# Moving three batches' 3x3 convolution and gate from the opening to the step ahead of the preceding batch's attention

## The chip, the cores and the metric

The kernel runs on one core of one Trainium2 chip. The metric is the time of one execution on the device in microseconds (us). Three executions of the kernel before took 5047.65, 5047.94 and 5053.58 us; the median is 5047.94 us.

## What is computed

The input x has 8 batches of 384 channels by 32x32 pixels (1024 tokens), all float32. Layer 0 normalizes each token over its channels (xn), runs a selective scan (a Mamba block) over the tokens forward and backward, and adds a gated depthwise convolution:

```
x_norm      = rmsnorm(x) * norm_w
global_feat = scale_mod * (mamba(x_norm) + flip(mamba(flip(x_norm))))
conv        = depthwise 3x3 convolution of x_norm            # per channel, over the 32x32 image
local_feat  = sigmoid(conv + dw_b) * x_norm
x           = x + res_scale * (global_feat + local_feat)
```

Layer 1 takes the tokens of that x through causal attention with 6 heads, and then, for batches 0 to 4, through a feed-forward block with sign-binarized weights whose activations are quantized with one maximum per batch. Only `local_feat` and the addition to x are computed in another place by the change.

## The kernel before, in words

A batch has 3 chunks of 128 channels (one channel per partition) and 2 halves of 512 tokens, so a tile of one chunk and half is 128x512 and fills one PSUM bank. PSUM's eight banks are handed out by tag: "s" and "pt" two each, "da" two, "y" and "av" one each (`BANKS`). Tiles of 128x1024 in SBUF come from a pool "mid" of 10 buffers, whole-batch tiles from a pool "big" of 6.

A batch passes through these stages:

- `before_scan` (L307): x is loaded (L320), normalized (L326 to L334), projected in `in_proj` (L336), convolved along the tokens in `conv` (L350) and passed through Silu; `local` (L383) makes the 3x3 convolution and `gates` (L444) the gate and the residual; `delta` (L511) makes the step sizes that the scan takes. Results are spilled to DRAM: u, us, z, "t" (x plus the local part) and the delta tiles.
- the scan: 96 units per batch (`Unit`, L544), each for two of the 16 states of one chunk, half and direction. A unit is a multiply on GpSimd (L588), two exponentials on ScalarE (L601), two scans on VectorE (L606), a second multiply on GpSimd (L612) and eight TensorE transposes that sum into PSUM (L620). `slot` (L1100) issues the parts of successive units, so that the first multiply of a unit is issued two slots ahead of its scans (`AHEAD`).
- `attention` (L674): loads of the scan's output and of "t", output projection (L695, added to "t" at L703), layer norm, q and k (L725), v (L743); from here on scores, softmax and weighted values; last the projection `ap` (L934). Up to and with v this text calls it the front of an attention.
- `feed_forward` (L968), for batches 0 to 4, spread together with `before_scan` of a batch still to come.

Every stage is a list of steps with a cost in us written by hand (`Steps`, L1074). `spread_over` (L1083) merges lists in proportion to the sums of their costs. First `before_scan` of batch 0 runs alone (`begin`, L1138). Then comes the opening: the slots of batch 0's 96 units are spread over one list, `beside` (L1137 to L1145), which holds batch 0's z projection and gates, the binarizing of both weights, and `before_scan` of batches 1, 2 and 3. Last comes the main part: the slots of the other seven batches are spread over `rest` (L1148 to L1157), in which follow for each batch its attention and its feed-forward; the due points of L1151 see to it that a batch's units are issued before its attention. After the last slot only the attention of batch 7 is left. From the lists a scheduler makes one fixed order per engine, and each engine takes its instructions in that order; `tc.high_priority` pulls some forward, `pin` keeps the order of some as written. All loads and spills named here are issued from SyncE's queue (`load`, L111; `spill`, L123), also in a fixed order.

For one chunk and half, `local` copies xn times the middle tap into a PSUM bank on ScalarE (L389) and adds the other eight taps with eight VectorE operations (L400), each reading and writing the bank. `gates` then applies tanh on ScalarE (L453), since sigmoid(v) = 0.5 + 0.5 tanh(v/2), and two VectorE operations: times xn (L460) and times half of res_scale plus x (L463).

In `local` and `gates` both halves of a chunk hold a bank of the tags "s" and "pt" in the opening, which the projections use too.

Of the kernel before, what the change touches and what calls it, by code (L numbers as in the profile page):

```python
# [22 lines left out]
NH = L // HB  # L23
# [20 lines left out]
HURRY = 400  # L44
AHEAD = 2
ORDER = (0, 1, 2, 3, 5, 6, 4, 7)
LOG_EXP = "natural_log_exp_and_others"


# [5 lines left out]
def kernel(  # L55
# [49 lines left out]
    def half(h):  # L105
        return slice(h * HB, (h + 1) * HB)
# [4 lines left out]
    def load(dst, src):  # L111
        nc.sync.dma_start(out=dst, in_=src)
# [10 lines left out]
    def spill(key, src, name):  # L123
        d = dram.tile([P, L], F32, name=name, tag="sp_" + "_".join(str(k) for k in key[1:]))
        nc.sync.dma_start(out=d, in_=src)
        spilled[key] = d
# [177 lines left out]
                    )  # L304


    def before_scan(b, tags, emit, later=None, diags=None):  # L307


        st = {}  # L310
# [2 lines left out]
        def bank_of(name):  # L313
            return bank(name, next(turns))
# [8 lines left out]
        for h in range(NH):  # L323

            @emit
            def _(h=h):  # L326
                sqs = squares(st["xn"], h, f"n0_{b}")
                ms = mean_of(lambda c: sqs[c], f"ms_{b}_{h}")
                rstd_of(ms, 0)
                for c in range(NC):  # L330
                    xc = st["xn"][:, c, half(h)]
                    nc.vector.scalar_tensor_tensor(
                        xc, xc, vec[:, c, V_NORM : V_NORM + 1], ms, ALU.mult, ALU.mult
                    )  # L334

        def in_proj(c, i, h):  # L336
            if i == 1 and h == 0:
# [42 lines left out]
                st["u", d, c][:, half(h)], acc, AF.Identity, bias=vec[:, c, V_CB : V_CB + 1]  # L380
            )

        def local(c, h):  # L383

            acc = bank_of(f"loc_{b}_{c}_{h}")
            r0, rows = h * (HB // W), HB // W
            img = acc.rearrange("p (i j) -> p i j", j=W)
            src = st["xn"][:, c, :].rearrange("p (i j) -> p i j", j=W)
            nc.scalar.activation(  # L389
                acc, st["xn"][:, c, half(h)], AF.Copy, scale=vec[:, c, V_DW + 4 : V_DW + 5]  # L390
            )
            for k in range(9):
                di, dj = k // 3 - 1, k % 3 - 1
                if k == 4:
                    continue
                i0, i1 = max(r0, -di), min(r0 + rows, H - di)
                j0, j1 = max(0, -dj), W - max(0, dj)
                to = img[:, i0 - r0 : i1 - r0, j0:j1]
                tap = src[:, i0 + di : i1 + di, j0 + dj : j1 + dj]
                nc.vector.scalar_tensor_tensor(  # L400
                    to, tap, vec[:, c, V_DW + k : V_DW + k + 1], to, ALU.mult, ALU.add
                )
            return acc
# [11 lines left out]
        for c in range(NC):  # L415

            @emit
            def _(c=c):
                st["up", c] = mtile(f"up_{b}_{c}")
                for d in range(2):  # L420
                    st["u", d, c] = mtile(f"u{d}_{b}_{c}")
                if c + 1 < NC:
                    weights_of(c + 1)

            for i, to in enumerate((emit, emit if later is None else later)):
                for h in range(NH):
                    to(lambda c=c, i=i, h=h: in_proj(c, i, h), 2.6)
            for d in range(2):
                for h in range(NH):
                    emit(lambda c=c, d=d, h=h: conv(c, d, h), 3.0)  # L430

            def silus(ts):
                for t in ts:
                    pin(nc.scalar.activation(t, t, AF.Silu))

            def sum_of_us(c=c):
                usum = mtile(f"us_{b}_{c}")
                nc.vector.tensor_tensor(usum, st["u", 0, c], st["u", 1, c], ALU.add)
                spill((b, "us", c), usum, f"sus_{b}_{c}")
                for d in range(2):  # L440
                    spill((b, "u", d, c), st["u", d, c], f"su_{d}_{b}_{c}")


            def gates(c=c, silus=silus, sum_of_us=sum_of_us):  # L444
                st["xc"] = mtile(f"xc_{b}_{c}")
                load(st["xc"], x[b, chunk(c), :])
                accs = [local(c, h) for h in range(NH)]
                with tc.high_priority(offset=60):
                    us = [st["u", 0, c], st["u", 1, c]] if later is None else []
                    silus(us + [st["z", c]])  # L450
                    for h in range(NH):
                        pin(
                            nc.scalar.activation(  # L453
                                accs[h], accs[h], AF.Tanh, scale=0.5, bias=dwbh[:, c : c + 1]
                            )
                        )
                    pin(nc.scalar.preload_act_table_set(LOG_EXP))
                for h in range(NH):
                    acc, xc = accs[h], st["xc"][:, half(h)]
                    nc.vector.scalar_tensor_tensor(  # L460
                        acc, acc, 1.0, st["xn"][:, c, half(h)], ALU.add, ALU.mult
                    )
                    nc.vector.scalar_tensor_tensor(xc, acc, rsh, xc, ALU.mult, ALU.add)  # L463
                spill((b, "t", c), st["xc"], f"st_{b}_{c}")
                spill((b, "z", c), st["z", c], f"sz_{b}_{c}")
                if later is None:
                    sum_of_us()

            def gates_of_us(c=c, silus=silus, sum_of_us=sum_of_us):
                with tc.high_priority(offset=60):  # L470
                    silus([st["u", 0, c], st["u", 1, c]])
                    pin(nc.scalar.preload_act_table_set(LOG_EXP))
                sum_of_us()

            if later is None:
                emit(gates, 14.0)
            else:
                emit(gates_of_us, 4.0)
                later(gates, 10.0)


            for h in range(NH):

                def project(c=c, h=h):
                    xp = bank_of(f"xp_{b}_{c}_{h}")
                    for d in range(2):
                        nc.tensor.matmul(
                            out=xp[d * DW : (d + 1) * DW, :],
                            lhsT=wx[:, c, :],
                            rhs=st["u", d, c][:, half(h)],  # L490
                            start=True,
                            stop=True,
                        )
                    xd = st["xd"][:, half(h)]
                    if c == 0:
                        nc.scalar.activation(xd, xp, AF.Identity, bias=onerow)
                    else:
                        nc.vector.tensor_tensor(xd, xd, xp, ALU.add)

                emit(project)  # L500
# [170 lines left out]
        spilled[b, "gy", c, h] = t  # L671


    def attention(b, emit_ffn, emit):  # L674
        st = {}

        @emit
# [55 lines left out]
        for j in range(NT):  # L733

            @emit
            def _(j=j):
                if j == 0:
                    st["v"] = btile(f"v_{b}").rearrange("p c l -> p (c l)").rearrange(
                        "p (j e) -> p j e", e=C
                    )  # L740
                vp = bank(f"vp_{b}_{j}")
                for c in range(NC):
                    nc.tensor.matmul(  # L743
                        out=vp[:, :C],
                        lhsT=st["xn"][:, c, chunk(j)],
                        rhs=wv[:, c, :],
                        start=(c == 0),
                        stop=(c == NC - 1),
                    )
                nc.any.tensor_copy(st["v"][:, j, :], vp[:, :C])  # L750

        @emit
        def _():
# [361 lines left out]
    def steps_of(stage, *args, **kwargs):  # L1115
        out = Steps()
        stage(*args, out, **kwargs)
        return out
# [19 lines left out]
    begin = Steps()  # L1138
    before_scan(ORDER[0], ("s", "pt"), begin, beside)
    run(begin)  # L1140
    beside += steps_of(before_scan, ORDER[1], ("s", "pt"), diags=diags)
    beside += steps_of(binarize, w1, w1s, NC, FF, 2, "w1")
    beside += steps_of(binarize, w2, w2s, NF, C, 8, "w2")
    for b in ORDER[2 : 1 + ahead]:
        beside += steps_of(before_scan, b, ("s", "pt"), diags=diags)  # L1145
    run(first, beside)

    rest, later, due = [], list(ORDER[1 + ahead :]), [(0.0, 0)]  # L1148
    for i, b in enumerate(ORDER):
        if i > 0:  # L1150
            due.append((sum(us for _, us in rest), i * per))  # L1151
        fed = Steps()
        rest += steps_of(attention, b, fed) if i < B - 1 else []
        if fed and later:
            fed = spread_over(fed, steps_of(before_scan, later.pop(0), ("pt", "pt", "av")))
            fed = [(f, JOINT * us) for f, us in fed]
        rest += fed  # L1157
# [65 lines left out]
```

## Time and profile before

| | us |
|---|---|
| median of three executions | 5047.94 |
| the profiled execution, whole | 5051.18 |
| its span, first to last instruction | 5049.4 |
| TensorE busy | 4101.8 |
| VectorE busy | 3599.9 |
| GpSimd busy | 3691.4 |
| ScalarE busy | 2721.4 |
| first scan multiply (L588) starts | 127 |
| first output projection of attention (L695) starts, batch 0 | 831 |
| the same, in the order of batches 1, 2, 3, 5, 6, 4, 7 | 1496, 2170, 2867, 3551, 3913, 4281, 4840 |
| first scores (L786) start, batches 0, 1, 2 | 924, 1610, 2284 |

The stretch 127 to 831 is the opening, 831 to 4840 the main part, and from 4840 on the last attention runs without scans. "Busy" is the time in which an engine executes, merged where instructions overlap. PE is TensorE's matmul, PEld its weight load, DVE VectorE, ACT ScalarE, POOL GpSimd and SP SyncE. L followed by a number is a line of the kernel before.

### The profile page before, as it was taken

How to read it: one execution, taken by the hardware profiler on the slowest of the kernel's cores; microseconds unless marked ns; L12 is line 12 of the kernel's file. 1: busy time of each engine (PE TensorE's matmuls, PEld its weight loads, DVE VectorE, ACT ScalarE, POOL GpSimd, SP SyncE). 2: the span in 40 equal slices, each digit the busy share in tenths (PEclk: the TensorE clock that was granted, in tenths of full speed). 3: DMA queues.
4: the chain of work that ended last, by engine and by line, in shares of the span. 5: the costliest groups of instructions: out<-in, count | busy, mean ns of one | idle time of the engine just before them, and what ended most of it. 6: DMA issues, size and time to landing. Idle time of an engine off the chain costs nothing. (4 is left out here: it accounts for less than half of the span.)

```text
span 5049.4 us, 50760 instructions
## 1 busy us (share of the span) xinstructions
PE 4101.8 (81%) x16458; PEld 2191.0 (43%) x16458; DVE 3599.9 (71%) x4780; ACT 2721.4 (54%) x4891; POOL 3691.4 (73%) x1944
## 2 busy tenths in 40 slices
PE   4687787878788888788787888888888978878899
PEld 1243343544434444444443444434444544444444
DVE  6887978667786777876678867678767666666523
ACT  4565665565645656545556446565365455464426
POOL 0578687987669886778876788768788978877710
PEclk7788797989889899888998889898888989989999
DMA  6554646324363334453234633335543334324210
GB/s 230 197 176 158 207 156 226 113 86 144 135 210 117 115 114 163 156 174 125 103 129 143 208 109 127 114 116 191 174 131 115 104 99 141 106 92 132 89 64 26
DMA packets 365010, 696.36 MB, mean 138 GB/s; under 512 B 30104, under 2 KB 88904, under 8 KB 364744
## 3 DMA queue, kind: packets, MB, share of 16 engines
q1 hardware_dynamic: 355232, 676.97, 39.7%
q10 hardware_dynamic: 9512, 16.15, 0.9%
q8 instruction: 130, 2.13, 0.2%
q14 instruction: 136, 1.11, 0.1%
HBM read 527.33 MB, written 165.68 MB: 137 GB/s over the span
## 5 line engine op out<-in xcount | busy, mean ns | idle before, releaser
L588 POOL TENSOR_TENSOR g<-ud,bc 128x1024 f32<-128x1024 f32 x768 | 1839.3, 2395 | 652.0 <-PE y L620 513.1
L612 POOL TENSOR_TENSOR g<-g,bc 128x1024 f32<-128x1024 f32 x768 | 1820.5, 2371 | 228.4 <-DVE g L606 175.6
L601 ACT ACTIVATE da<-dl,amat 128x512 f32<-128x512 f32 x1536 | 1056.1, 691 | 1481.1 <-DVE g L606 1438.6
L606 DVE TENSOR_TENSOR_SCAN g<-da,carry,g 128x512 f32<-128x512 f32 x768 | 957.6, 1271 | 405.7 <-POOL g L588 364.7
L606 DVE TENSOR_TENSOR_SCAN g<-da,g 128x512 f32<-128x512 f32 x768 | 906.4, 1210 | 472.7 <-POOL g L588 439.9
L620 PE MATMUL y<-ident,g 128*128 128x128 f32 x6144 | 932.4, 299 | 270.7 <-POOL g L612 214.6
L620 PEld LDWEIGHTS y<-ident,g 128*128 128x128 f32 x6144 | 772.5, 154 | 729.1 <-POOL g L612 339.9
L786 PE MATMUL s<-k,q 64*128 64x512 f32 (+3 forms) x1152 | 405.1, 610 | 122.9 <-DVE nm L800 111.5
L800 DVE CUSTOM_DVE_ANT_0 pr<-s,cmask 128x512 f32<-128x512 f32 (+3 forms) x576 | 300.6, 545 | 212.6 <-PE s L786 185.8
L810 ACT ACTIVATE pr<-pr,nm 128x512 f32<-128x512 f32 (+3 forms) x576 | 348.8, 606 | 141.7 <-DVE nm L800 139.5
L862 PE MATMUL pt<-ident,pr 128*128 128x128 f32 x1728 | 301.9, 305 | 73.5 <-ACT ptn L864 32.9
L993 PE MATMUL hp<-t,w 128*128 128x512 f32 x720 | 339.4, 617 | 27.1 <-DMA w<-w1s 15.2
L1038 PE MATMUL yp<-h,w 128*128 128x512 f32 x720 | 329.2, 615 | 10.3 <-DMA w<-w2s 5.5
L341 PE MATMUL in<-xn,win 128*128 128x512 f32 x576 | 293.3, 651 | 46.3 <-DVE xc L463 14.8
L862 PEld LDWEIGHTS pt<-ident,pr 128*128 128x128 f32 x1728 | 209.1, 153 | 237.2 <-ACT ptn L864 88.6
L875 PE MATMUL av<-ptn,v 128*64 128x512 f32 (+3 forms) x1152 | 276.6, 563 | 23.9 <-DVE o L889 16.2
L864 ACT COPY ptn<-pt 128x512 f32<-128x512 f32 (+3 forms) x576 | 255.2, 474 | 74.0 <-PE pt L862 72.6
L725 PE MATMUL qp<-t,wqk 128*128 128x512 f32 x576 | 263.9, 608 | 17.5 <-DVE t L302 12.0
L400 DVE SCALAR_TENSOR_TENSOR loc<-xn,vec,loc 128x496 f32<-128x496 f32 (+3 forms) x384 | 260.4, 721 | 24.2 <-ACT loc L389 22.7
L611 POOL COPY carry<-g 128x2 f32<-128x2 f32 x384 | 85.8, 224 | 248.1 <-DVE g L606 248.1
L786 PEld LDWEIGHTS s<-k,q 64*128 64x128 f32 x1152 | 138.4, 208 | 251.8 <-DVE nm L800 187.6
L1038 PEld LDWEIGHTS yp<-h,w 128*128 128x128 f32 x720 | 140.3, 199 | 178.9 <-issue 166.3
(155 smaller groups left out, 4809.8 us busy)
## 6 DMA issues: line engine op xcount, KB each, us to landing
bc<-rows SPq DMA_DIRECT2D x512, 512.0 KB, 4.1
dl<-sdl SPq DMA_DIRECT2D x160, 256.0 KB, 2.9
ud<-sud SPq DMA_DIRECT2D x160, 256.0 KB, 2.7
t<-st SPq DMA_DIRECT2D x63, 512.0 KB, 5.3
su<-u SPq DMA_DIRECT2D x48, 512.0 KB, 3.8
du<-su SPq DMA_DIRECT2D x96, 256.0 KB, 4.5
sdl<-du SPq DMA_DIRECT2D x96, 256.0 KB, 2.4
sud<-du SPq DMA_DIRECT2D x96, 256.0 KB, 2.8
```

The costliest lines, as they stand in the source:

```text
L341: nc.tensor.matmul(out=mp, lhsT=st["win", c][:, k, i, :], rhs=st["xn"][:, k, half(h)], start=(k == 0), stop=(k == NC - 1),)
L588: pin(nc.gpsimd.tensor_tensor(g, ud, sst["bc", 0, u.b, u.part, u.n], ALU.mult))
L601: nc.scalar.activation(da, sst["dl", u.b, u.c, u.part], AF.Exp, scale=amat[:, u.c, n : n + 1])
L606: nc.vector.tensor_tensor_scan(gi[:, ::step], da[:, ::step], gi[:, ::step], first, ALU.mult, ALU.add)
L612: pin(nc.gpsimd.tensor_tensor(g, g, sst["bc", 1, u.b, u.part, u.n], ALU.mult))
L620: nc.tensor.matmul(out=y[:, j, :], lhsT=g[:, i, chunk(j)], rhs=ident, is_transpose=True, start=(u.opens and i == 0 and j == 0), stop=(u.cl ...
L786: mm = nc.tensor.matmul(out=ss[e][:, : k1 - k0], lhsT=st["q"][rows_of(e), c, chunk(qi)], rhs=st["k"][rows_of(e), c, k0:k1], start=True, st ...
L800: nc.vector.tensor_tensor_reduce(out=x, in0=ss[e][:, :w], in1=mask, scale=-1.0, scalar=-MASKED, op0=ALU.add, op1=ALU.min, accum_out=m,)
L810: nc.scalar.activation(x, x, AF.Exp, bias=m, scale=-1.0, accum_out=rs[:, i, e, kb : kb + 1])
L862: nc.tensor.transpose(pt[:, chunk(i)], pr[:, e, chunk(j % QT)], ident)
L993: nc.tensor.matmul(out=hp, lhsT=st["w1"][:, c, chunk(m % 2)], rhs=st["xn"][:, c, half(h)], start=(c == 0), stop=(c == NC - 1),)
L1038: nc.tensor.matmul(out=yp, lhsT=st["w2", k // 6][:, k % 6, :], rhs=st["h", k // NC][:, k % NC, half(h)], start=(k == 0), stop=(k == NF - 1),)
```

## The change

`before_scan` gets a list `apart`, given for batches 1, 2 and 3. For these, the opening keeps only a step of cost 5.0 per chunk in place of 14.0 (`gates_of_all`: the Silus, and the spills of z, us and u), and after the second half is normalized the three chunks of xn are spilled. The convolution, the gate and the residual become six steps of cost 4.0 per batch (`gates_apart`, one for each chunk and half). They are spread over the front of the attention of the batch before (batch 0's attention takes those of batch 1, and so on). There xn and x are loaded again, the bank comes from the tag "av", and the sigmoid is made as exp(-ln(1 + exp(-v))), with v held above -64 by one more VectorE operation. Batch 0 and the four later batches keep the old form.

```diff
+                    if apart is not None and h == NH - 1:
+                        spill((b, "xn", c), st["xn"][:, c, :], f"sxn_{b}_{c}")
...
+            def gates_apart(c, h):
+                if h == 0:
+                    st["xa"], st["xc"] = mtile(f"xa_{b}_{c}"), mtile(f"xc_{b}_{c}")
+                    load(st["xa"], spilled[b, "xn", c])
+                    load(st["xc"], x[b, chunk(c), :])
+                acc = bank(f"loc_{b}_{c}_{h}", "av")
+                local(acc, st["xa"], c, h)
+                nc.vector.tensor_scalar(
+                    acc, acc, vec[:, c, V_DWB : V_DWB + 1], LOWEST, ALU.add, ALU.max
+                )
+                nc.scalar.activation(acc, acc, AF.Exp, scale=-1.0)
+                nc.scalar.activation(acc, acc, AF.Ln, bias=onecol)
+                nc.scalar.activation(acc, acc, AF.Exp, scale=-1.0)
+                nc.vector.tensor_tensor(acc, acc, st["xa"][:, half(h)], ALU.mult)
+                xc = st["xc"][:, half(h)]
+                nc.vector.scalar_tensor_tensor(xc, acc, sc[:, 1:2], xc, ALU.mult, ALU.add)
+                if h == NH - 1:
+                    spill((b, "t", c), st["xc"], f"st_{b}_{c}")
+
+            def gates_of_all(c=c, silus=silus, sum_of_us=sum_of_us):
+                with tc.high_priority(offset=60):
+                    silus([st["u", 0, c], st["u", 1, c], st["z", c]])
+                    pin(nc.scalar.preload_act_table_set(LOG_EXP))
+                spill((b, "z", c), st["z", c], f"sz_{b}_{c}")
+                sum_of_us()
+
-            if later is None:
+            if apart is not None:
+                emit(gates_of_all, 5.0)
+                for h in range(NH):
+                    apart(lambda c=c, h=h: gates_apart(c, h), 4.0)
+            elif later is None:
                 emit(gates, 14.0)
...
+        if beside:
+            emit[:] = spread_over(emit, beside[:len(beside)])
...
-    beside += steps_of(before_scan, ORDER[1], ("s", "pt"), diags=diags)
+    apart = {b: Steps() for b in ORDER[1 : 1 + ahead]}
+    beside += steps_of(before_scan, ORDER[1], ("s", "pt"), diags=diags, apart=apart[ORDER[1]])
...
-        beside += steps_of(before_scan, b, ("s", "pt"), diags=diags)
+        beside += steps_of(before_scan, b, ("s", "pt"), diags=diags, apart=apart[b])
...
-        rest += steps_of(attention, b, fed) if i < B - 1 else []
+        if i < B - 1:
+            rest += steps_of(attention, b, fed, beside=apart.get(ORDER[i + 1], ()))
```

## The prediction, written before the changed kernel ran

> **What bounds the kernel now.** I read the busy time of the engines by stage first, since the change takes work out of one stage and puts it into three others. The columns are the stretch, its length, then busy us of PE, PEld, DVE, ACT and POOL with their instructions, the granted clock, the share of DMA time and GB/s. The rows shown are the opening, front, scores part and rest (feed-forward beside a later batch's preparation) of attention 0, then fronts and rests of attentions 1 and 2.
>
> ```profile
> core 0: us, PE busy (x) PEld busy (x) DVE busy (x) ACT busy (x) POOL busy (x), PEclk, DMA share, GB/s
> 127.00:831.00 704.00, 519.29 (x1599) 260.11 (x1600) 601.48 (x677) 418.85 (x625) 503.69 (x258) 0.80 0.55 187
> 831.00:924.00 93.00, 88.99 (x299) 47.57 (x298) 57.95 (x64) 34.94 (x56) 83.89 (x54) 0.96 0.43 148
> 924.00:1117.00 193.00, 155.51 (x831) 88.61 (x829) 138.67 (x246) 121.58 (x288) 171.12 (x86) 0.86 0.30 102
> 1117.00:1496.00 379.00, 314.10 (x1119) 164.31 (x1118) 289.29 (x322) 214.84 (x312) 266.60 (x142) 0.89 0.46 154
> 1496.00:1610.00 114.00, 97.21 (x334) 51.57 (x333) 81.05 (x89) 46.56 (x76) 97.55 (x48) 0.94 0.44 149
> 1829.00:2170.00 341.00, 288.65 (x940) 150.83 (x938) 273.81 (x306) 194.39 (x275) 249.88 (x128) 0.88 0.48 163
> 2170.00:2284.00 114.00, 98.72 (x333) 53.52 (x333) 82.58 (x93) 46.26 (x74) 98.54 (x50) 0.92 0.41 137
> 2522.00:2867.00 345.00, 281.34 (x925) 144.90 (x924) 271.58 (x301) 193.35 (x272) 249.26 (x130) 0.89 0.45 152
> ```
>
> In the opening DVE is busy 601.5 of 704 (85%), PE 74%, POOL 72%. In the three fronts DVE is the idle one (62%, 71%, 72%) while POOL has 90%, 86%, 86%. The rests lie between: DVE 76 to 80%, PE 82 to 85%. In every stage PE, DVE and POOL together are busy 2.3 to 2.5 times its length: where one has room another does not.
>
> The waits of the opening say whom DVE keeps waiting (who waited for whom, us in total, times, longest):
>
> ```profile
> POOL carry L611 <- DVE g L606: 123.4, 13, 49.1
> ...
> PEld dp L518 <- DVE du L527: 51.7, 22, 12.7
> POOL g L612 <- DVE g L606: 38.8, 6, 18.8
> ...
> DVE loc L400 <- ACT loc L389: 17.5, 9, 2.5
> PEld in L341 <- DVE xc L463: 16.3, 4, 6.7
> ```
>
> POOL stood 162 us for scans that were queued on DVE behind other work, once for 49 us; PE waited for the banks that the gate holds (L463). DVE itself waits little. So the opening is DVE's, and what leaves DVE there is late work.
>
> The instructions of the local step within the opening (columns: DVE busy, ACT busy, clock, DMA):
>
> ```profile
> 127.00:831.00 704.00, 161.28 (x240) 32.10 (x48) 0.80 0.55 187
> ```
>
> 240 is 24 halves of ten DVE operations: the 18 that leave and batch 0's six that stay. One half is 161.28/24 = 6.72 us of DVE and 1.34 us of ACT.
>
> **What the Trainium skill says.** "Perfetto Trace Analysis", section "Identifying the Most-Contended Engine", takes occupancy as the measure for Vector, Scalar and GpSimd, and the section after it advises interleaving regimes that have different contended engines; the table above shows two such regimes. "ScalarE: Activation LUTs", section "Table sets", puts exp and ln into one set, so the new sigmoid needs no table load of its own; the trace loads that set with 1.28 us each time, and the built order has 126 loads against 124, so loads are neither saved nor added. "GPSIMD Engine Reference", section "Specifications", names contention with DVE instructions that have two SBUF inputs; the local taps have one (the other is PSUM), and POOL's L588 takes 2.50 us in the opening with them and 2.38 later, so I charge POOL nothing in the fronts.
>
> **The change, part by part.**
>
> 1. Removed from the opening: 18 halves of 6.72 = 121.0 us of DVE and 24 us of ACT. DVE falls to 480.5, beside PE 519.3 and POOL 503.7. Were DVE the sole bound at its 85%, the gain would be 704 x 121.0/601.5 = 142 us, but PE and POOL are next. If PE reaches the best share of a long mixed stage, 288.65/341 = 0.846, the opening takes 614 us (gain 90). If the three together reach what the rests reach (2.30, 2.38, 2.32; mean 2.33), it takes (519.3 + 480.5 + 503.7)/2.33 = 645 (gain 59). I take the middle, 75. What is late next is POOL in the stretches of projections and PE everywhere.
>
> 2. Slots: the list beside the opening loses 9 x 9 = 81 us of its cost, so the same 96 units are spread over less: more of them now fall into the delta stretches, where DVE is full. This is in the 75: it is why I don't go to 90.
>
> 3. Added to the fronts, DVE: a half is 6.72 plus the new reset to -64, for which I take L1066, the nearest two-scalar operation (743 ns; a read from PSUM could make it 0.68): 7.46. Six are 44.8 us per front, 134 in all. The product and residual keep their price (L460's 685 and L463's 736 ns).
>
> 4. Added slots in the fronts: each `rest` front grows by 24 us of cost and draws units from later stages. The built order of DVE has 21.5, 26.5 and 27.5 units of scans between the first output projection and the first score, against 16, 23 and 23: 13.5 more, of about 2.4 us DVE each and 2.40 + 2.37 us POOL each. DVE's work in the fronts becomes 58.0 + 44.8 + 13.2 = 116, 81.1 + 44.8 + 8.4 = 134 and 82.6 + 44.8 + 10.8 = 138. At the highest share DVE reached in a stretch of the opening (115.12 of 126 us, 0.91, from 505 to 631) they last 128, 147 and 152 us, against 321 now: +106. POOL's pace gives the same: 62 units of 4.77 us at 0.88 are 336, and DVE's 427 sets it.
>
> 5. Given back elsewhere: the 13.5 units no longer lie in scores parts and rests. POOL's pace in a scores part is 171.12/4.77 = 36 units in 193 us, 5.4 us a unit; in a rest they share with others, so I take 4.5: 13.5 x 4.5 = 61. Parts 3 to 5 together: +45. The bounds: 0, if POOL hid all of it, and 134/2.3 = 58 by the sum of three engines, with +106 if nothing is given back.
>
> 6. ACT: 18 halves lose a tanh (0.66) and gain exp, ln, exp (L269, L268, L269 before: 0.57 + 0.65 + 0.57 = 1.79): +20 us, and each front gets 6 x 2.48 = 15 us on an engine busy 38 to 41%. Cost nothing on throughput. As a wait it counts: the product after the third activation stands in DVE's fixed order with scans queued behind it, and POOL's second multiply waits for those. The built order lays zero to four other DVE instructions (up to some 4 us) over about 2 us of activations. From the trace: L460 waited 2.2 us in all for tanh. Bounds 0 and 18 x 4 = 72; I take 0.
>
> 7. SP and DMA: 9 spills of xn added in the opening, where 9 loads of x and 9 spills of t leave; in the fronts 9 loads of xn come with the 9 loads and 9 spills moved. Two more transfers of 512 KB for each chunk, 9.4 MB: at 677 MB in 39.7% of 5049 us that is 28 us of all engines' time over shares of 0.41 to 0.55, covered. On SP's queue a spill of xn waits for the normalization, with row loads for later units behind it; those run two to four slots (10 to 20 us) ahead. The bank "av" serializes halves: 9 to 12 us each, six in 130 to 150 us, covered. I take 0; bounds -5 to +15. Leaving "s" and "pt" frees PE's 16 us wait at L341, inside part 1.
>
> Sum: -75 + 45 = -30. The profiled execution took 5051.2 (span 5049.4), 3.2 above the median; taken off the median 5047.9 this is 5018.
>
> **The rivals.**
>
> A, the sum above: 5018. With -60 to -90 in the opening and +30 to +60 later its own range is 4988 to 5048.
>
> B, the fronts hide it: POOL sets their pace, DVE's idle 99 us (35 + 33 + 31) take most of the 134, main +15; opening -90. 5048 - 75 = 4973. For it: POOL's 86 to 90% there. Against: 138 us of DVE don't fit into 114.
>
> C, no net: the sum of three engines holds in both places, -59 and +58: 5047. For it: that sum barely varies over the stages.
>
> D, slower: DVE stands at the product (part 6) in each of the 18 halves, scans behind it. With w us each the result is -30 + 18w; it is slower than before by 0.2% from w = 2.2 on, and at w = 3.4 it is +31: 5079. For it: ACT's exponentials of the scan stand between the three activations in the built order, and ACT already waits 49.8 us for scans in front 0. Against: the scheduler laid other instructions over most of them.
>
> That the move doesn't happen is excluded: the built order has the 144 taps within the fronts.
>
> **How the numbers follow.** A measurement tells about 0.2% (10 us) from no change. Chances: A 0.47, B 0.24, C 0.10, D 0.19. Faster: B, and A without its upper fifth: 0.62. Same: most of C and A's end: 0.17. Slower: D and a little of C: 0.21. For 8 in 10 the range goes from 4950 (B with an opening PE runs at a higher clock than 0.80) to 5070 (most of D).
>
> **What would show it.** Right: attention 0's output projection starts near 756 instead of 831; POOL's wait at L611 for scans in the opening falls by half; fronts of about 128, 147 and 152 us with DVE near 0.9; the stretch between the two marks 831 and 4840 longer by 45. Wrong in step 1: an opening over 650 with DVE under 75%. Wrong in steps 3 to 5: fronts as short as before (B), or DVE idle in them for activations (D). Wrong altogether if the main part's scans stall in stages that the change doesn't touch.

## The result, and the profile after

The changed kernel takes 5064.75 us (median of seven executions, 5055.56 to 5072.82), the kernel before 5049.68 on the same chip (seven, 5047.15 to 5053.58). The ratio is 1.0029, 95% interval 1.0019 to 1.0039: slower by 0.29%, some 15 us. The forecast was 5018.

One caution on reading the traces: the profiled execution of the changed kernel is its fastest, 5055.56 with a span of 5053.8; that of the kernel before is 5051.18 with 5049.4. So the two traces show 4.4 of the 15 us. The other 10 are in no trace here; the changed kernel's executions scatter over 17 us, those of the kernel before over 6 here and over 14 to 23 in the longer series beside the experiments. Lengths of stretches below are those of one trace each: the openings of six kernels with nearly the same opening list (the changed kernel, experiments 1 to 3 and both of 4) are 683 to 687, so a difference of 4 us says nothing.

The lines moved by up to 40 in the changed kernel. The ones used below: L623 and L647 are the scan's first and second multiply on POOL (before L588, L612), L646 the carry (L611), L641 the scan (L606), L655 the matmuls on y (L620), L401 the taps (L400), L487 the new reset, L490 to L492 the three activations, L493 the product, L560 to L563 the delta arithmetic (L525 to L528).

By stage (columns as in the first fence of the prediction): opening, the fronts of attentions 0, 1 and 2, and the main part.

```profile
127.00:810.00 683.00, 510.88 (x1607) 260.95 (x1608) 483.77 (x502) 393.87 (x588) 508.80 (x261) 0.79 0.55 189
810.00:924.00 114.00, 94.44 (x336) 51.52 (x334) 99.94 (x123) 55.17 (x90) 100.13 (x61) 0.95 0.47 157
1467.00:1606.00 139.00, 104.95 (x366) 56.38 (x366) 125.08 (x151) 67.18 (x110) 117.69 (x54) 0.90 0.48 164
2176.00:2316.00 140.00, 106.97 (x364) 57.48 (x363) 120.09 (x149) 63.01 (x102) 116.07 (x64) 0.90 0.45 153
810.00:4845.00 4035.00, 3316.56 (x13895) 1802.29 (x13893) 2956.69 (x3955) 2192.03 (x4017) 3176.06 (x1660) 0.90 0.40 134
```

DVE's work left the opening as the prediction said: 601.5 to 483.8 us. But the opening went only from 704 to 683: DVE is now busy 71% of it instead of 85%, PE and POOL 75% and 74%, about what they had before (74% and 72%). The engine that looked like the bound was relieved of a fifth of its work, and nobody took up the room. The main part grew by 26 (4009 to 4035), the fronts alone by 72 (321 to 393). -21 + 26 is the 5 us of the traces.

### Where the opening's 54 us are

The prediction expected -75 in the opening. Two of the largest waits within it, 127 to 810 (who waited for whom, us in total, times, longest):

```profile
DVE g L641 <- POOL g L623: 146.8, 65, 5.4
...
POOL carry L646 <- DVE g L641: 71.3, 8, 40.9
```

POOL's wait at the carry fell from 123 to 71, nearly by the half that was foreseen, and DVE's for POOL's first multiply rose from 67 to 147. DVE, done early, now waits for POOL. To see where, the opening must be cut where its work changes. The projections of a batch are PE work with the gates; after them its "delta" steps are DVE work. A delta stretch is cut here from its first matmul (L518, after the change L553) to about the first work of the next batch. The kernel before, delta stretches and projections in turn:

```profile
349.00:412.00 63.00, 38.72 (x84) 16.95 (x84) 62.90 (x71) 44.60 (x76) 32.84 (x13) 0.59 0.67 223
412.00:564.00 152.00, 122.36 (x419) 63.51 (x420) 114.44 (x129) 81.12 (x113) 131.70 (x72) 0.88 0.44 150
564.00:622.00 58.00, 38.63 (x86) 17.57 (x84) 56.86 (x65) 39.87 (x70) 29.31 (x16) 0.58 0.67 227
622.00:763.00 141.00, 119.38 (x416) 62.72 (x417) 114.49 (x125) 81.56 (x112) 122.00 (x56) 0.93 0.48 168
763.00:831.00 68.00, 38.53 (x122) 20.78 (x121) 63.57 (x72) 41.32 (x72) 41.19 (x22) 0.62 0.72 247
```

The same five of the changed kernel:

```profile
338.00:396.00 58.00, 38.57 (x94) 19.56 (x94) 47.71 (x54) 36.53 (x65) 33.96 (x14) 0.55 0.59 200
396.00:542.00 146.00, 122.91 (x420) 63.42 (x419) 87.47 (x83) 80.94 (x112) 136.06 (x73) 0.89 0.49 163
542.00:608.00 66.00, 37.20 (x113) 21.10 (x111) 54.69 (x56) 39.04 (x69) 45.32 (x26) 0.57 0.55 177
608.00:726.00 118.00, 110.44 (x358) 54.73 (x358) 74.47 (x68) 67.59 (x95) 92.83 (x39) 0.96 0.55 190
726.00:810.00 84.00, 43.59 (x162) 26.25 (x162) 63.31 (x75) 42.26 (x72) 52.62 (x27) 0.64 0.67 232
```

DVE's 85% was an average of two kinds of stretch. Before, it had 93 to 100% in the delta stretches, and only 75% and 81% in the two projections, which held 96 of the 144 taps that leave; there POOL already stood at 87% and PE at 80 and 85%. Taking the 18 halves away lowered DVE to 60 and 63% in the projections. In the first, POOL rose to 93%: a gain of 6 us in 152. The second gained 23 us; there POOL has 79% and PE 94%, with 39 POOL instructions instead of 56. The projections became shorter by 29 us together, the delta stretches longer by 19, since scan units that left the projections went into them; ahead of the first delta stretch another 11 were gained.

The delta work itself did not grow. From a batch's first L526 (after the change L561) to its last DVE takes 150 us for the three batches together, in both kernels. But the first comes 16, 21 and 22 us after the stretch's first matmul, against 5, 9 and 7 before. These delays, in the changed kernel:

```profile
338.00:354.00 16.00, 13.65 (x47) 8.43 (x47) 10.68 (x11) 9.19 (x16) 16.00 (x8) 0.67 0.46 161
542.00:563.00 21.00, 13.42 (x47) 9.03 (x45) 11.24 (x11) 10.38 (x18) 20.68 (x13) 0.56 0.48 155
726.00:748.00 22.00, 13.59 (x76) 10.05 (x76) 11.73 (x12) 9.98 (x18) 19.32 (x9) 0.77 0.54 189
```

POOL is busy 56 of these 59 us: the projections end earlier, but scan units stand in the fixed orders ahead of the delta work, and they go at POOL's pace. The delta work starts only 1, 7 and 22 us earlier than before. Where exactly a stretch is cut changes the 29 and the 19, not their direction.

One hole is left untouched by the change. A line of POOL's timeline in the changed kernel (start, length, then in brackets how long it had stood and for whom):

```profile
209.21 0.19 POOL L646 COPY carry<-g 128x2 f32<-128x2 f32 x1 [40.87 <-DVE g L641]
```

From 168.3 to 209.2 POOL stands: batch 0's own taps (old form, most of the 48 run on DVE from 168.8 to 206) lie ahead of the scan that POOL waits for.

### The profile page after: what moved, and what is told of

The parts are those of the page before. It is cut to its first block, busy times and chain, and to the rows that moved or that the text cites. A ratio compares the mean times of both kernels' runs of the same rounds, so it can differ in the third digit from the quotient of the medians.

```text
span 5053.8 us, 50909 instructions
## 1 busy us (share of the span) xinstructions
PE 4077.6 (81%) x16458; PEld 2177.7 (43%) x16458; DVE 3588.6 (71%) x4785; ACT 2744.6 (54%) x4942; POOL 3693.2 (73%) x1944
## 5 line engine op out<-in xcount | busy, mean ns | idle before, releaser
L623 POOL TENSOR_TENSOR g<-ud,bc 128x1024 f32<-128x1024 f32 x768 | 1839.0, 2395 | 626.8 <-PE y L655 461.9
L647 POOL TENSOR_TENSOR g<-g,bc 128x1024 f32<-128x1024 f32 x768 | 1825.8, 2377 | 271.6 <-DVE g L641 135.6
L641 DVE TENSOR_TENSOR_SCAN g<-da,carry,g 128x512 f32<-128x512 f32 x768 | 956.5, 1271 | 455.9 <-POOL g L623 401.3
L641 DVE TENSOR_TENSOR_SCAN g<-da,g 128x512 f32<-128x512 f32 x768 | 911.3, 1211 | 462.5 <-POOL g L623 422.0
L655 PE MATMUL y<-ident,g 128*128 128x128 f32 x6144 | 940.5, 300 | 315.5 <-POOL g L647 231.9
L655 PEld LDWEIGHTS y<-ident,g 128*128 128x128 f32 x6144 | 772.8, 154 | 766.5 <-POOL g L647 359.1
L646 POOL COPY carry<-g 128x2 f32<-128x2 f32 x384 | 81.8, 213 | 232.6 <-DVE g L641 232.6
L1032 PEld LDWEIGHTS hp<-t,w 128*128 128x128 f32 x720 | 135.4, 196 | 192.0 <-issue 158.7
```

The costliest lines, as they stand in the source:

```text
L623: pin(nc.gpsimd.tensor_tensor(g, ud, sst["bc", 0, u.b, u.part, u.n], ALU.mult))
L641: nc.vector.tensor_tensor_scan(gi[:, ::step], da[:, ::step], gi[:, ::step], first, ALU.mult, ALU.add)
L647: pin(nc.gpsimd.tensor_tensor(g, g, sst["bc", 1, u.b, u.part, u.n], ALU.mult))
L655: nc.tensor.matmul(out=y[:, j, :], lhsT=g[:, i, chunk(j)], rhs=ident, is_transpose=True, start=(u.opens and i == 0 and j == 0), stop=(u.cl ...
L1032: nc.tensor.matmul(out=hp, lhsT=st["w1"][:, c, chunk(m % 2)], rhs=st["xn"][:, c, half(h)], start=(c == 0), stop=(c == NC - 1),)
```

## The experiments

Theory 1: the moved work lay where POOL already bound, so taking it out frees little, and what is left of the opening's loss are its holes, the start stall and the delta stretches (1b). Theory 2: something that the change added eats the gain, the transfers first of all; for the holes, that each one filled is replaced by another wait (2b). Theory 3: the opening's gain is real but lost again later, so that a shorter opening doesn't bring an earlier end. For the main part: VectorE work in the fronts against the units drawn into them. Attention 0's output projection starts at 831 before and 810 after; the main part from there to the last attention's lasts 4009 and 4035. The kernel before took 5048.6 to 5050.2 beside these runs; ratios are to it. Diffs are against the changed kernel, except where one says against the kernel before.

### 1. The moved work left out altogether

```diff
-                    if apart is not None and h == NH - 1:
-                        spill((b, "xn", c), st["xn"][:, c, :], f"sxn_{b}_{c}")
...
-                    load(st["xa"], spilled[b, "xn", c])
                     load(st["xc"], x[b, chunk(c), :])
-                acc = bank(f"loc_{b}_{c}_{h}", "av")
-                local(acc, st["xa"], c, h)
...
-                nc.vector.scalar_tensor_tensor(xc, acc, sc[:, 1:2], xc, ALU.mult, ALU.add)
```

> The changed kernel with the convolution, gate and residual of batches 1, 2 and 3 left out altogether (x itself is spilled as t), without the spills and loads of xn. Theory 1 (the opening's stretches of projections are paced by GpSimd, its delta stretches by the order on VectorE, so the freed VectorE time idles): attention 0's output projection starts at 800 to 812 us, hardly before the changed kernel's 810, the main part lasts about as long as before the change (4009), whole time about 5030. Theory 2 (the release was worth its 75 us, and the spills of xn and the traffic they hold up took it back): output projection near 755, whole time near 4975.

Measured: 5046.98, ratio 1.0000 (0.9990 to 1.0011). Its opening and main part:

```profile
127.00:814.00 687.00, 508.05 (x1599) 258.92 (x1600) 483.78 (x497) 392.46 (x585) 506.28 (x261) 0.79 0.53 179
814.00:4836.00 4022.00, 3317.84 (x13902) 1807.02 (x13902) 2847.67 (x3772) 2146.37 (x3935) 3176.19 (x1660) 0.90 0.40 133
```

With 18 halves of convolution, sigmoid and residual done nowhere, DVE has 109 us less in the main part than the changed kernel, and the kernel is no faster than before. The opening gains 17, about what the move gained (21). Even with a main part as before this would be 17 us, not 30; the theory's 5030 was still too low, since the main part is 13 longer than before with no local work in it. That is taken up in 4.

### 2. Only the transfers kept

```diff
-                acc = bank(f"loc_{b}_{c}_{h}", "av")
-                local(acc, st["xa"], c, h)
                 nc.vector.tensor_scalar(
-                    acc, acc, vec[:, c, V_DWB : V_DWB + 1], LOWEST, ALU.add, ALU.max
+                    st["xc"][:, h : h + 1], st["xa"][:, h : h + 1], 1.0, None, ALU.mult
                 )
...
-                nc.vector.scalar_tensor_tensor(xc, acc, sc[:, 1:2], xc, ALU.mult, ALU.add)
```

> The changed kernel with the spills of xn and the loads of xn and x kept, but the convolution, gate and residual of batches 1, 2 and 3 left out (one column per half is copied, to keep the loads). Theory 1: within 8 us of the kernel that leaves the transfers out too, about 5030. Theory 2: the transfers cost the opening some 50 us, so it begins attention 0 near 805 while the kernel without transfers begins near 755.

Measured: 5046.93, ratio 0.9996 (0.9987 to 1.0006), against 5046.98 without the transfers; the opening is 687 in both. The spills and loads move (188 GB/s in the opening instead of 179) and cost nothing that can be measured. Theory 2 falls for the transfers.

### 3. The three activations left out

```diff
-                nc.scalar.activation(acc, acc, AF.Exp, scale=-1.0)
-                nc.scalar.activation(acc, acc, AF.Ln, bias=onecol)
-                nc.scalar.activation(acc, acc, AF.Exp, scale=-1.0)
```

> The changed kernel with exp, ln and exp of the moved gates left out (the product takes the convolution itself). The prediction's part 6: these activations hide, so the time stays within 5 of the changed kernel, 5058 to 5066. Rival D: VectorE stands for them at the product in 18 halves, so at least 15 us come off: 5048 or less.

Measured: 5066.27, ratio 1.0030 (1.0018 to 1.0042), the same as with them; opening 686, main part 4033. In the changed kernel the product's own row and its wait say it too:

```profile
L493 DVE TENSOR_TENSOR loc<-loc,xa x18: 668/674/700, 823.9 to 2340.2; 128x512 f32<-128x512 f32 x18
...
  ACT loc L492: 2.6, 3
```

DVE waited 2.6 us in all, three times in 18 halves, for the activations. Rival D's 15 us are not there.

### 4. The main part: work against units drawn

The first takes the six steps' cost down, so that they draw nearly no scan units into the fronts:

```diff
-                    apart(lambda c=c, h=h: gates_apart(c, h), 4.0)
+                    apart(lambda c=c, h=h: gates_apart(c, h), 0.2)
```

> The changed kernel with the cost of each moved step in the list at 0.2 in place of 4.0, so that the same work stands in the fronts but draws no scan units to them. If the main part's loss (4035 against 4009 us) comes from the units drawn into the fronts, half of which was seen without any convolution there, it falls by about 13: whole time about 5048. If it comes from VectorE's work in the fronts, it stays: about 5062, or more, since the same work then has less time.

Measured: 5084.56, ratio 1.0079 (1.0066 to 1.0092), with an opening of 684 and a main part of 4058. That is above both expectations. The units drawn were a help: without them the main part is 49 longer than the 4009 of before, with them 26.

The second is the same edit on experiment 1's kernel, where there is no work either:

```diff
-                    apart(lambda c=c, h=h: gates_apart(c, h), 4.0)
+                    apart(lambda c=c, h=h: gates_apart(c, h), 0.2)
```

> The convolution, gate, residual and transfers of xn of batches 1, 2 and 3 left out as in the first kernel of the study, and the moved steps' cost set to 0.2, so that no units are drawn to the fronts either. If units drawn to fronts without work there cost the main part its 13 us (4022 against 4009), the main part is 4009 again and the whole time about 5032. If the main part is longer for another reason, it stays at 5047.

Measured: 5055.28, ratio 1.0008 (1.0000 to 1.0016), opening 685. Its main part:

```profile
812.00:4845.00 4033.00, 3328.79 (x13902) 1810.01 (x13901) 2839.72 (x3772) 2153.50 (x3938) 3173.31 (x1660) 0.90 0.40 133
```

This was expected near 4009. With neither the convolution nor its units, the main part is still 24 longer than before, 20 of it between the output projections of attentions 1 and 2 (674 to 695), and there in the scores part and the rest (9 and 10 us), not in the front. All kernels here that change the list of the main part have one of 4017 to 4058, the two that don't (5 and 7 below, on the kernel before) have 4007 and 4010. What does it in the order of the instructions stays open. As differences of main parts: the work costs 25 without units (4058 against 4033) and 13 with them (4035 against 4022). The medians of whole times say 29 and 18.

The fronts alone answer another question, what makes them long. In experiment 1's kernel they hold no local work but the drawn units:

```profile
814.00:927.00 113.00, 98.01 (x340) 54.26 (x340) 67.61 (x71) 42.25 (x68) 103.16 (x62) 0.91 0.47 157
1471.00:1604.00 133.00, 103.10 (x364) 56.65 (x364) 91.30 (x97) 54.47 (x88) 116.81 (x54) 0.91 0.49 161
2169.00:2300.00 131.00, 104.82 (x367) 56.12 (x366) 92.87 (x104) 48.58 (x75) 116.44 (x65) 0.93 0.47 157
```

They last 377 us, with DVE at 60 to 71%, nearly as long as the 393 of the changed kernel. The fronts of the two kernels with the cost at 0.2 last 345 with the work and 321 without, and those of the kernel before 321. So 56 of the fronts' 72 us come with the units drawn, which other stages are then spared, and 16 with DVE's work.

### 5. Delta steps spread over the next batch's preparation

If DVE's delta stretches hold up POOL, their steps laid evenly beside the next projections should fill the holes. First on the changed kernel:

```diff
-                emit(lambda c=c, d=d, h=h: delta(c, d, h), 3.0)
+                (emit if deltas is None else deltas)(lambda c=c, d=d, h=h: delta(c, d, h), 3.0)
...
-        beside += steps_of(before_scan, b, ("s", "pt"), diags=diags, apart=apart[b])
+        of_last, left = left, Steps()
+        more = steps_of(before_scan, b, ("s", "pt"), diags=diags, apart=apart[b], deltas=left)
+        beside += spread_over(more, of_last)
+    beside += left
```

> The changed kernel with the 12 delta steps of batch 1 spread over the preparation of batch 2, those of batch 2 over that of batch 3; batch 3's stay last in the opening. Theory 1: two of three stretches in which GpSimd starves go, each worth about 30 us, because VectorE has room in the projections now; attention 0 begins near 750, whole time about 5000. Theory 2: where the deltas stand makes no difference, whole time within 10 of the changed kernel, 5055 to 5065.

Measured: 5046.66, ratio 0.9996 (0.9988 to 1.0004); 18 us less than the changed kernel's median. The opening:

```profile
127.00:800.00 673.00, 508.19 (x1607) 254.18 (x1608) 517.46 (x504) 405.85 (x599) 517.26 (x261) 0.81 0.56 193
```

A gain of 10 in the opening, not 60. The same edit on the kernel before (without `apart`):

```diff
-        beside += steps_of(before_scan, b, ("s", "pt"), diags=diags)
+        of_last, left = left, Steps()
+        more = steps_of(before_scan, b, ("s", "pt"), diags=diags, deltas=left)
+        beside += spread_over(more, of_last)
+    beside += left
```

> The kernel before the change with the deltas of batches 1 and 2 spread in the same way. Theory 1: VectorE has little room in the projections here (601 us of work; at its best share of 0.91 it needs 660), so less is gained than by the same edit on the changed kernel: attention 0 begins near 800 instead of 831, whole time about 5020. Theory 2: no difference, about 5050.

Measured: 5066.68, ratio 1.0037 (1.0024 to 1.0049): slower. The opening:

```profile
127.00:851.00 724.00, 517.51 (x1599) 257.64 (x1600) 616.62 (x676) 441.01 (x642) 508.60 (x258) 0.80 0.54 182
```

The sign was missed. The same edit takes 10 from an opening in which DVE has room, and adds 20 where it has not. The moved work did make room on DVE; the changed kernel doesn't use it.

### 6. The delta steps of batches 1 to 3 left out

```diff
             for c in range(NC):
+                if diags is not None:
+                    for what in ("dl", "ud"):
+                        spilled[b, what, d, c, h] = spilled[ORDER[0], what, d, c, h]
+                    continue
                 emit(lambda c=c, d=d, h=h: delta(c, d, h), 3.0)
```

> The changed kernel with the delta steps of batches 1, 2 and 3 left out (their scans read batch 0's delta tiles). Theory 1b: the three stretches of 50 to 75 us, in which GpSimd gets through 4 to 7 units, are what is left of the opening's loss; without them 100 units run at 4.87 us behind the start's stall: attention 0 begins near 690 instead of 810, and since the main part has the same work, the whole time falls as much, to about 4945. Rival 3 (what the opening gains the main part takes back, since scans started earlier wait for other things there): attention 0 begins earlier, but the whole time falls by less than half of that, to 5000 or more.

Measured: 4955.57, ratio 0.9806 (0.9793 to 0.9820). Opening and main part:

```profile
127.00:711.00 584.00, 448.02 (x1551) 235.12 (x1552) 372.74 (x360) 326.71 (x457) 510.27 (x267) 0.86 0.52 177
711.00:4736.00 4025.00, 3318.66 (x13878) 1809.65 (x13876) 2950.86 (x3951) 2190.05 (x4014) 3168.07 (x1654) 0.90 0.40 134
```

The opening loses 99 us, and the median (of four executions) lies 109 below the changed kernel's: this gain of the opening goes through whole, so theory 3 is out, but for the 13 to 24 us of main part that experiments 1 and 4 leave without a cause. Compare the two removals. About 118 us of DVE work taken out of projections and start (601.48 - 483.77) brought 17 to 21 us. About 111 us taken out with the delta steps (483.77 - 372.74) brought 99, and left POOL the fullest engine, busy 87% of the opening (510.27 of 584; PE 77%). This kernel also leaves out the deltas' matmuls and activations, and with 36 steps of cost 3.0 gone the list spreads the units differently, so how much of the 99 is DVE's isn't shown.

### 7. Batch 0's convolution moved as well

The start stall is batch 0's own. Its six halves in the new form, spread over batch 2's preparation (the first mark of a cut stands for batch 0's z, whose Silu and spill stay a step of their own):

```diff
...
-    before_scan(ORDER[0], ("s", "pt"), begin, beside)
+    apart0 = Steps()
+    before_scan(ORDER[0], ("s", "pt"), begin, beside, apart=apart0)
...
-        beside += steps_of(before_scan, b, ("s", "pt"), diags=diags, apart=apart[b])
+        more = steps_of(before_scan, b, ("s", "pt"), diags=diags, apart=apart[b])
+        beside += spread_over(more, apart0) if b == ORDER[2] else more
```

> The changed kernel with batch 0's convolution, gate and residual moved too: its xn is spilled, and the six steps are spread over batch 2's preparation in the opening, in the new form. Theory 1b (the opening is paced by GpSimd where VectorE has room, and what is left of its loss is where long runs of VectorE work stand ahead of the scans: 41 us at 168 to 209, batch 0's taps, and the three delta stretches): the wait of 41 us goes, attention 0 begins near 772 instead of 810, whole time near 5025. Rival 2b (GpSimd's stall at the start is made up later, since slots are spread over the whole opening and its end is set by the last preparation): attention 0 begins within 8 us of 810, whole time about 5060.

Measured: 5052.66, ratio 1.0008 (1.0000 to 1.0016); opening 671, a gain of 12 instead of the expected 38. The taps had been in DVE's way, but behind them stood the next late item: between 150 and 240 DVE now stands 13.4 us at a normalization of batch 1 (L334) for ACT, then 10.0 us at a product (L439) for the Silu, each with scans behind it. Over the opening POOL still waits 65.8 us at the carry.

With the edit of 5 beside it:

> The two edits together on the changed kernel: batch 0's local part late, the deltas of batches 1 and 2 spread over the next preparation. Theory 1b: the gains add, attention 0 begins near 762, whole time near 5010. Rival 2b: as the changed kernel with spread deltas alone, about 5047.

Measured: 5046.50, ratio 0.9996 (0.9987 to 1.0005); opening 673. The two gains, 12 and 10, don't add, as 2b said.

Alone on the kernel before (batches 1 to 3 keep their convolution in the opening):

> The kernel before the change, but with batch 0's local part moved as above (spread over batch 2's preparation), the gates of batches 1, 2 and 3 left in the opening. Theory 1b: the start's wait goes (49 us before), but the 47 us of VectorE work move into a stretch where VectorE is at 75 to 100%, so part of it comes back: attention 0 begins near 810, whole time about 5030. Rival 2b: attention 0 begins near 831, about 5050.

Measured: 5045.15, ratio 0.9994 (0.9986 to 1.0003); opening 701, main part 4007. Three us of the opening are no gain that one trace can show: 2b, replacement by the next wait, holds for the start stall.

### 8. The moved steps spread over the whole attention

The fronts are short and full; the stretch from front to the end of the scores is about three times as long. Experiment 5's first kernel, with the six steps spread over front and scores and the bank taken from "pt":

```diff
-                acc = bank(f"loc_{b}_{c}_{h}", "av")
+                acc = bank(f"loc_{b}_{c}_{h}", "pt")
...
-        if beside:
-            emit[:] = spread_over(emit, beside[:len(beside)])
...
         emit.extend(waiting)
+        if beside:
+            emit[:] = spread_over(emit, beside[:len(beside)])
```

> The changed kernel with the deltas of batches 1 and 2 spread, and the six moved steps spread over the front and the scores part of the attention instead of the front alone, with banks from pt. If VectorE's 0.9 in the fronts is what the main part pays for, it spreads to about 0.78 over 320 us, and the whole time falls from that kernel's 5047 to about 5030. Rival: the step holds one of the two pt banks for 12 us or more, which the transposes of the scores part need, and the time rises above 5055.

Measured: 5036.85 (eleven executions), ratio 0.9976 (0.9966 to 0.9986): faster than both kernels, by 12 us than before and by 28 than the changed one. Of the 28, 18 are experiment 5's; against that kernel, its own base, the median falls by 10, not by the expected 17. The rival, a stall for the bank, is out. Opening and main part:

```profile
127.00:796.00 669.00, 506.79 (x1598) 252.24 (x1599) 514.99 (x497) 405.75 (x598) 512.92 (x258) 0.81 0.56 191
796.00:4818.00 4022.00, 3344.82 (x13905) 1824.65 (x13904) 2952.70 (x3960) 2195.77 (x4018) 3180.36 (x1663) 0.90 0.40 135
```

The trace puts 4 of the 10 into the opening and 5 into the main part (4022 against its base's 4027). In fronts 0 and 1 DVE falls to 67% and 83% (91% and 89% in the base), and they shrink from 110 and 139 to 103 and 119. But the stages behind grow: from attention 0's output projection to attention 3's this kernel takes 2065 us (796 to 2861), and so does its base (800 to 2864). The 5 us lie between the output projections of attentions 3 and 5, where none of the six steps stand. So DVE's work was made thinner in the fronts, and no gain is seen where this was done; where the 10 us come from stays open, also because the bank's tag was changed together with the place. That the work is hidden isn't shown either: no run left it out of this arrangement.

## Why the prediction was wrong

**Step 1 failed:** "I take the middle, 75". Measured 21. The term was read from averages over a stage of 704 us. The prediction concluded that "the opening is DVE's" because "DVE itself waits little"; its own table of waits has DVE 66.7 us for POOL's first multiply, in a row that it left out. Where the work lay, POOL had 87%, PE 80 to 85% and DVE 75 to 81%. The sum of three engines that the prediction trusted at 2.33 isn't a law: it fell from 2.31 to 2.20 ((510.88 + 483.77 + 508.80)/683), since the units went on at POOL's pace. Even the lower bound, 59, was no bound. That POOL and PE would be late next the prediction did say, but it left them room that the stretches don't have. Its own mark, "an opening over 650 with DVE under 75%", came true with 683 and 71%. Experiment 1 shows it: the work left out altogether is worth 17 us of opening. Experiment 5 shows that DVE got room that goes unused, and experiment 6 that the opening gives way when the delta steps go.

**Step 2** named the cause on the way, slots falling into delta stretches, and counted it as small. POOL's instructions there rose from 51 (13 + 16 + 22) to 67 (14 + 26 + 27), and these stretches grew by 19 us while the projections shrank by 29: two thirds of the projections' gain. DVE is no longer full in them (82, 83 and 75%); they begin with units at POOL's pace.

**Step 3** held in its size: the reset takes 734 ns against 743 taken, and front 0 has 40.2 us of local work on DVE for 56 of its 66 instructions, 7.9 us a half at that rate against 7.46; the rest lie just outside.

**Step 4** came out in kind, but not by its mechanism. The fronts last 114, 139 and 140 with DVE at 88, 90 and 86%, +72. The expected lengths were 128, 147 and 152, +106, from DVE at 0.91. But without DVE's local work they still last 113, 133 and 131 (experiment 4): the units drawn set the length. The prediction set POOL's pace beside it with 62 units, the number of before; with the 75.5 that it expected the same sum gives 409 us, and with the 70.5 that came 382. Units drawn were 11.5, not 13.5 (17.5 to 21, 21 to 25, 20.5 to 24.5, counted by POOL's multiplies), and DVE's work in the fronts came to 345 us instead of 388.

**Step 5**, given back 61: measured 46 (26 - 72). Steps 3 to 5 together were +45 and came out +26 in the trace. The ledger of experiment 4 shows that this is no single cost: in the traces 13 from the work itself, the other 13 from a main part that is longer with no local work in it. That one stays without a cause. In the second kernel of experiment 4 most of it lies in a scores part and a rest without moved work, which is the prediction's mark "wrong altogether", at a size of 20 us.

**Steps 6 and 7** held: activations (experiment 3) and transfers (experiment 2) cost nothing that can be measured.

**The rivals.** The end was D's, slower, and 5065 lies in D's span of 5058 to 5079, but without D's mechanism: w was not 2.2 us but 2.6/18 = 0.14. D's number is luck. C, no net, is 18 us off, and its reason, that the sum of engines holds in both places, is refuted by the opening's 2.20. B was right that POOL sets the fronts' pace; but it left out the units drawn, and its gain of 90 in the opening failed with step 1.

What stays open: the main part's 13 to 24 us that come with the changed list, the 10 us of experiment 8, and the 9 us by which the changed kernel's median lies above its profiled execution.

## What to carry to other kernels

Before costing the removal of work, cut the stage into stretches in which the mix of work is one, and read each engine's share in the stretch where that work lies: an engine at 85% on average may be at 75% just there, beside another at 87%. A run with the work left out is a cheap estimate of what any move of it can bring; here the whole time stayed the same, while leaving out other steps, with 111 us of the same engine and some work of two more, took 99 us from the opening. And count what a move draws with it: the fronts grew by 72 us, of which 56 came with the scan units that the moved steps' cost drew there, and only 16 with the moved work.

## What was unexpected of the hardware

DVE instructions with two inputs in SBUF stretch beside a running POOL, and POOL's stretch with them. Timelines of DVE and of POOL in a delta stretch of the changed kernel (DVE's in groups of two; L560 and L562 read a PSUM tile, L561 and L563 two tiles in SBUF):

```profile
380.36 1.28 DVE L560 SCALAR_TENSOR_TENSOR du<-dp,du 128x512 f32<-128x512 f32 x2
381.56 4.42 DVE L561 SCALAR_TENSOR_TENSOR dp<-ew 128x512 f32<-128x512 f32 x2
...
390.48 1.29 DVE L561 SCALAR_TENSOR_TENSOR dp<-ew 128x512 f32<-128x512 f32 x2
```

```profile
380.00 2.65 POOL L647 TENSOR_TENSOR g<-g,bc 128x1024 f32<-128x1024 f32 x1 [13.46 <-DVE g L641]
382.61 2.81 POOL L623 TENSOR_TENSOR g<-ud,bc 128x1024 f32<-128x1024 f32 x1
```

The same line takes 4.42 us for two while POOL multiplies and 1.29 while POOL stands (it stands from 385.4 to 400.9); POOL's multiply of 128x1024 takes 2.65 to 2.81 us here, and 2.35 before it (at 353.2) and after it (at 405.8). L560 beside the running POOL keeps its 1.28. This agrees with the Trainium skill, "GPSIMD Engine Reference", section "Specifications", which names contention between GpSimd and VectorE instructions with two SBUF inputs; the size is this trace's. The prediction applied the section to the taps, which have one such input, and not to the delta steps. It doesn't explain the result: L561 and L563 took 104 us of DVE in the opening after the change, and L526 and L528 took 111 before it.
